# Row normalization in one ScalarE pass, gains moved to GpSimd and to the transposed copies (two-layer graph transformer, 1 core)

## Chip, core and metric

The kernel runs on one core of one Trainium2 chip. The metric is the device time of one execution in microseconds (us); smaller is better. Engines are named as in the profile: PE is TensorE (PEld its weight loads), DVE is VectorE, ACT is ScalarE, POOL is GpSimd, SP is SyncE.

## What is computed

Two layers of a graph transformer over 2708 nodes with 512 features, 8 heads of 64 and a hidden width of 2048. `x` is 2708x512, `adj` a 0/1 matrix of 2708x2708, very sparse; all values are float32. Each layer is

```
q, k, v = h @ Wq.T + bq, h @ Wk.T + bk, h @ Wv.T + bv
scores  = per head q.k / 8, and -1e9 where a node is no neighbour
ctx     = softmax(scores) @ v
h1 = layer_norm(h + ctx @ Wo.T + bo)  * ln1_g + ln1_b
h2 = layer_norm(h1 + relu(h1 @ W1.T + b1) @ W2.T + b2) * ln2_g + ln2_b
```

and `layer_norm(z)` is `(z - mean) / sqrt(variance + 1e-5)` along a row. `h2` of layer 0 is `h` of layer 1; `h2` of layer 1 is the result.

## The kernel before, in words

**Tiles and blocks.** The nodes stand in 22 tiles of 128 rows (the last has 20), ordered by how many neighbours they have. A layer works on 11 blocks of two tiles each (called blocks 0 to 10 here), in the order of the list `blocks`; the tile of 20 rows is in block 10.

**Attention** works on lists of neighbours. Keys and values of a node are one row of 1024 numbers in a DRAM table. For each neighbour slot of a tile POOL issues one indirect DMA that fetches 128 such rows (L1114, `kv<-kv_d`), into a small ring of buffers. Two slots make a chunk of attention: DVE multiplies by the queries (L1151) and sums per head (L1157, tile `sc`), ACT takes the exponential (L1170, `p<-sc`) and scales the values of one slot head by head (L1177, 8 instructions), DVE scales the other slot (L1183) and adds both to the sum (L1190). At the end of a tile ACT divides, again in 8 instructions (L1221, tile `cx`).

**Dense work** goes block by block. `attended` turns `cx` with PE, multiplies by Wo, adds the residual and normalizes: tiles `h`. `turned` transposes `h` with PE into PSUM (`flip`, tile `tp`) and ACT copies it out, adding the shift as a bias per column (L1341, `hT`). `feed_forward` (layer 0: blocks 0, 1 and 10; all of layer 1) and `feed_forward_by_seven` (layer 0: blocks 2 to 9, seven products instead of eight for W2, with partial sums of W2 in the tiles `forms`) go through the hidden width in 16 pieces, called steps 0 to 15 here: four matmuls into `pf` (L1578, L1720), a Relu by ACT into `ft` or `forms` (L1589, L1731), products with W2 three steps (or two pairs of steps) later. The result plus `h` is `z`.

**Normalization.** Most tiles use the class `Norm`. DVE adds and sums a row (`total`, L1294) and makes the negative mean `nm` (L1305). ACT squares the centred row and sums the squares (`squares`, L1311). `centred` has POOL compute the reciprocal deviation `rd` (L1318, L1320: two instructions of 128x1) while DVE forms `(z + nm) * gain` (L1321, 128x512). `scaled` has ACT multiply the row by `rd` (L1327, 128x512). The shift of the row that is kept for the residual is added by an accumulating DMA that POOL issues (`added_row`, L1330). The function `norm` does the same with other instructions, mostly on DVE, for the `h` of the first block of a layer (in layer 0 the first two) and the `z` of the last.

**What sets the order.** The order is written by hand in the loop over steps at the end of the file. While block k goes through its 16 steps, the end of block k-1 is worked off as `tail` (the generator `ended`; the table `TAILS` names the steps at which it moves on) and, in layer 0, as `behind` (`keys_values`: at step 7 the two `z` are turned and copied out as `zT`, at steps 8 and 9 the keys and values of layer 1 are projected from `zT`, L621 `k` and `v`, then the rows go to DRAM). At step 2 the shift is added to the `h` of block k. At steps 10 to 14 the next block's `attended` runs, at step 15 its `turned`. `advance` moves attention ahead by an amount that a table sets for each step. Each engine runs its instructions strictly in this written order. In layer 0, from block 2 on, `TAILS` gives the steps 3, 4, 5 and 6: squares of the first tile at 3, of the second at 4, `centred` at 5, `scaled` at 6, right ahead of the turning at 7.

**The end of layer 1.** Before the last steps of the last block the kernel makes sure that its lists held all neighbours: 22 small POOL copies (L1096, tile `checks`) at step 8, six small DVE instructions up to `held` (L1896), and at step 12 a small matmul of `held` (L1899), which stands in PE's order between the matmuls of that block. Otherwise a slower version of the whole program would run; in the runs here it doesn't.

Of the kernel before, what the change touches and what calls it, by code (L numbers as in the profile page):

```python
# [13 lines left out]
ALU = mybir.AluOpType  # L14
# [41 lines left out]
TAILS = ((0, 1, 5, 6), (3, 4, 5, 6), (0, 1, 2, 3, 5, 8))  # L56
# [428 lines left out]
def by_edges(ctx: ExitStack, tc: tile.TileContext, x, xT, adj, layers, out, redo):  # L485
# [780 lines left out]
    def norm(z, r, gain, shift=None, st=None):  # L1266
# [9 lines left out]
        nc.gpsimd.tensor_tensor(rd[:r], va[:r], mhalf[:r], ALU.pow)  # L1276
        nc.vector.scalar_tensor_tensor(
            z[:r], z[:r], mv[:r, 0:1], gain[:r], ALU.subtract, ALU.mult
        )
        if shift is None:  # L1280
            nc.vector.tensor_scalar(z[:r], z[:r], rd[:r], None, ALU.mult)
            return
        nc.vector.scalar_tensor_tensor(z[:r], z[:r], rd[:r], shift[:r], ALU.mult, ALU.add)

    class Norm:


        def __init__(self, z, r, gain, junk):
            self.z, self.r, self.gain, self.junk = z, r, gain, junk
# [25 lines left out]
        def centred(self):  # L1315
            r, z, nm = self.r, self.z, self.nm
# [4 lines left out]
            nc.vector.scalar_tensor_tensor(  # L1321
                z[:r], z[:r], nm[:r], self.gain[:r], ALU.add, ALU.mult
            )

        def scaled(self):
            r, z = self.r, self.z
            nc.scalar.activation(z[:r], z[:r], AF.Copy, scale=self.rd[:r])  # L1327
# [4 lines left out]
    def flip(z, r, to, shift=None):  # L1332
# [7 lines left out]
        for c in range(NC):  # L1340
            nc.scalar.activation(  # L1341
                to[:, c, :], tp[:, c, :r], AF.Identity, bias=shift[:, c : c + 1]
            )

    class Layer:
# [5 lines left out]
        def load_first(self):  # L1351
# [7 lines left out]
            self.unsettled = raw_columns(w, ("bv", "ln1_b"), place)  # L1359
            self.bv, self.e1 = [col[0] for col in self.unsettled]  # L1360
# [44 lines left out]
        def load_next(self):  # L1405
# [4 lines left out]
            self.unsettled += raw_columns(self.w, ("ln2_b",), place)  # L1410
            self.e2c = self.unsettled[-1][0]
# [64 lines left out]
        def attended(self, block, got, xbs=None, soon=False):  # L1476
# [16 lines left out]
            for i, xb in enumerate(xbs):  # L1493
# [8 lines left out]
                if soon:  # L1502
                    if self.n == 0 and block == blocks[0]:
                        nc.vector.tensor_tensor(h[:r], h[:r], self.bo[:r], ALU.add)
                    norm(h, r, self.g1)
                else:
                    norms.append(Norm(h, r, self.g1, xb).total(parts[-1], last))
# [6 lines left out]
            for one in norms:  # L1514
                one.centred()
# [5 lines left out]
        def turned(self, block, hs):  # L1521
            hT = dn.tile([P, NC, 2 * P], F32, tag="hT", name="hT", bufs=1)
            c0 = 0
            for g, h in zip(block, hs):
                r = size(g)
                flip(h, r, hT[:, :, c0 : c0 + r], self.e1)
# [3 lines left out]
        def feed_forward(self, block, hs, hT):  # L1530
# [81 lines left out]
            for g, a, h in zip(block, accs, hs):  # L1612
# [15 lines left out]
                else:  # L1628
                    zs.append(Norm(z, r, self.g2, a).total(a[:r], h[:r]))
                    continue  # L1630
                norm(z, r, self.g2, self.e2 if apart else None, st)
# [43 lines left out]
        def feed_forward_by_seven(self, k, block, hs, hT):  # L1675
# [93 lines left out]
            yield [Norm(z, P, self.g2, u34).total(a, z) for z, a in ((zA, a0), (zB, a1))]  # L1769
# [413 lines left out]
```

## Time and profile before

| | |
|---|---|
| two runs | 1835.44 and 1838.9 us, median 1837.17 us |
| profiled execution | 1834.85 us, of which the traced span is 1833.1 us |
| TensorE clock granted | 0.999 of full speed |
| busy in the span | PE 1807.7 us, DVE 1327.7, ACT 1050.6, POOL 919.3 |
| gathers of keys and values by POOL (L1114) | 420, 509.7 us busy |
| normalizing passes of DVE (L1321) | 78 |
| normalizing passes of ACT (L1327) | 78 |

A row of the timeline gives start, length, engine, line, operation, out<-in, the shapes and the count of what is merged in it; in brackets stands how long the engine had been idle before it and what ended that. Queue rows such as POOL's DMA instructions cost the engine's time as well.

### The profile page before, as it was taken

What the parts mean: (1) busy time and instruction counts of PE and PEld (TensorE: products, weight loads), DVE (VectorE), ACT (ScalarE), POOL (GpSimd) and SP (SyncE); (2) the same over time, 40 slices, a digit from 0 to 9 for tenths busy, and PEclk for the clock granted to TensorE, in tenths of its full rate; (3) what the DMA queues carried; (4) which work ended last, traced back from release to release, by engine and by line L of the source; (5) the groups of instructions that cost most, each with busy time, mean ns of one, the idle gap of its engine ahead of it and who ended that gap; (6) DMA issues with size and microseconds to landing.
All of it is one profiled execution on the core that took longest, in us unless ns stands there. A gap on an engine that the chain in (4) does not pass through costs nothing.

```text
span 1833.1 us, 22912 instructions
## 1 busy us (share of the span) xinstructions
PE 1807.7 (99%) x6563; PEld 1161.2 (63%) x6563; DVE 1327.7 (72%) x2271; ACT 1050.6 (57%) x3505; POOL 919.3 (50%) x929
## 2 busy tenths in 40 slices
PE   9999999999999999999999999999999999999998
PEld 4444456566777867767686644666666666666666
DVE  5986768876969778697775147867797787788732
ACT  5770436655656556565664213666676676677641
POOL 3234756645645556365551132454574566567512
PEclk9999999999999999999999999999999999999999
DMA  9997988867878787686863786955675685666511
GB/s 343 376 335 258 370 271 275 240 205 254 263 221 243 239 240 241 201 253 202 248 198 113 230 288 263 321 155 195 213 238 169 228 261 176 220 208 204 154 29 38
DMA packets 172943, 420.73 MB, mean 230 GB/s; under 512 B 19258, under 2 KB 62638, under 8 KB 172808
## 3 DMA queue, kind: packets, MB, share of 16 engines
q0 software_dynamic: 85488, 279.03, 49.1%
q1 hardware_dynamic: 77162, 118.55, 18.7%
q10 hardware_dynamic: 10158, 21.61, 3.1%
q8 instruction: 53, 0.87, 0.2%
q14 instruction: 82, 0.67, 0.1%
HBM read 338.78 MB, written 53.44 MB: 214 GB/s over the span
## 4 chain that ended last, share of the span: by engine, by line
PE 80%; issue 6%; DVE 5%; DMA 3%; ACT 3%; POOL 3%; POOLq 0%; SPq 0%; DVEq 0%; ACTq 0%
PE pf L1578 17%; PE a L1551 17%; PE pf L1720 8%; PE k L621 7%; PE v L621 7%; PE o L621 7%; PE q L621 5%; PE c L1710 4%; PE a L1710 3%; PE tp L1336 2%; DVE kv L1151 1%; ACT kv L1177 1%; DVE sc L1157 1%; POOL kv L1114 1%; DMA kv<-kv_d,listed 1%
## 5 line engine op out<-in xcount | busy, mean ns | idle before, releaser
L1114 POOL DMA_INDIRECT kv<-kv_d,listed x420 | 509.7, 1214 | 282.4 <-issue 108.3
L1578 PE MATMUL pf<-hT,w 128*128 128x256 f32 (+1 forms) x1792 | 393.1, 367 | 0.8 <-ACT ft L1589 0.7
L1578 PEld LDWEIGHTS pf<-hT,w 128*128 128x128 f32 x1792 | 323.5, 190 | 104.4 <-issue 61.0
L1551 PE MATMUL a<-w,ft 128*128 128x512 f32 x800 | 373.5, 592 | 0.1
L1177 ACT ACTIVATE kv<-kv,p 128x64 f32<-128x64 f32 x1232 | 311.0, 335 | 5.0
L1151 DVE TENSOR_TENSOR kv<-kv,q 128x1024 f32<-128x1024 f32 (+1 forms) x222 | 257.4, 1159 | 18.5 <-DMA q<-q_d,ident_i 11.7
L1157 DVE TENSOR_REDUCE sc<-kv 128x16 f32<-128x1024 f32 (+1 forms) x222 | 258.0, 1162 | 7.6
L1190 DVE TENSOR_TENSOR acc<-acc,kv 128x1024 f32<-128x1024 f32 (+2 forms) x178 | 206.3, 1159 | 58.6 <-ACT kv L1177 45.8
L1720 PE MATMUL pf<-hT,w 128*128 128x256 f32 x1024 | 232.9, 379 | 0.0
L1551 PEld LDWEIGHTS a<-w,ft 128*128 128x128 f32 x800 | 150.0, 190 | 113.0 <-issue 102.0
L1720 PEld LDWEIGHTS pf<-hT,w 128*128 128x128 f32 x1024 | 193.9, 190 | 33.3 <-issue 8.1
L1318 POOL TENSOR_SCALAR va<-sq 128x1 f32<-128x1 f32 (+1 forms) x78 | 38.2, 490 | 314.6 <-ACT xb L1311 219.5
L1170 ACT ACTIVATE p<-sc,listed 128x8 f32<-128x8 f32 x420 | 104.0, 296 | 127.8 <-DVE sc L1157 105.6
L1589 ACT ACTIVATE ft<-pf,b 128x256 f32<-128x256 f32 (+1 forms) x208 | 94.6, 458 | 105.3 <-PE pf L1578 96.6
L621 PE MATMUL o<-wo,cT 128*128 128x512 f32 x336 | 150.8, 592 | 0.0
L1183 DVE TENSOR_TENSOR kv<-kv,p 128x512 f32<-128x512 f32 (+1 forms) x178 | 123.2, 692 | 8.0 <-ACT p L1170 7.8
L1294 DVE CUSTOM_DVE_ANT_0 h<-o,xb 128x512 f32<-128x512 f32 x36 | 24.9, 691 | 129.1 <-PE o L621 105.9
L621 PEld LDWEIGHTS o<-wo,cT 128*128 128x128 f32 x336 | 63.6, 190 | 73.2 <-issue 66.5
L1731 ACT ACTIVATE ft<-pf,b 128x256 f32<-128x256 f32 x96 | 44.8, 466 | 100.0 <-PE pf L1720 95.2
L746 DVE MAX8 tops<-code 128x8 f32<-128x247 f32 (+2 forms) x242 | 78.6, 400 | 27.2 <-ACT code L741 27.2
L1330 POOL DMA_DIRECT2D h<-ln_b x86 | 83.6, 1114 | 24.5 <-PE tp L1336 21.8
L1221 ACT ACTIVATE cx<-acc,su 128x64 f32<-128x64 f32 (+1 forms) x352 | 88.3, 333 | 11.8 <-DVE su L1213 8.9
(246 smaller groups left out, 2477.2 us busy)
## 6 DMA issues: line engine op xcount, KB each, us to landing
aj<-in_adj SPq DMA_DIRECT2D x42, 677.0 KB
forms<-form_d SPq DMA_DIRECT2D x168, 128.0 KB
h<-ln_b POOLq DMA_DIRECT2D x83, 256.0 KB
kv_d<-kvs ACTq DMA_DIRECT2D x21, 512.0 KB
xg<-in_xT SPq DMA_DIRECT2D x19, 512.0 KB
w<-in_W SPq DMA_DIRECT2D x16, 512.0 KB
kv<-kv_d,listed POOLq DMA_INDIRECT x420
zT_d<-zT SPq DMA_DIRECT2D x22, 256.0 KB
```

What stands on the lines that cost most here:

```text
L621: nc.tensor.matmul(o[:r], xs(c), wm[:, c, :], start=(c == 0), stop=(c == NC - 1))
L1114: return nc.gpsimd.indirect_dma_start(out=to, out_offset=None, in_=table[:, :], in_offset=bass.IndirectOffsetOnAxis(ap=s, axis=0), bounds_ ...
L1151: nc.vector.tensor_tensor(kv[:r, :c, :DM], kv[:r, :c, :DM], self.q[:r].unsqueeze(1).to_broadcast([r, c, DM]), ALU.mult,)
L1157: nc.vector.tensor_reduce(self.sc[:r, s0 : s0 + c, :], kv[:r, :c, :DM].rearrange("p s (h d) -> p s h d", d=DK), AX.X, ALU.add,)
L1170: nc.scalar.activation(p[:r, s, :], self.sc[:r, s, :], AF.Exp, bias=minus[:r, g, s : s + 1])
L1177: nc.scalar.activation(to[:, i, hd], kv[:r, i, DM + h * DK : DM + (h + 1) * DK], AF.Copy, scale=p[:r, s0 + i, h : h + 1],)
L1183: nc.vector.tensor_tensor(to[:, 0, :].rearrange("p (h d) -> p h d", d=DK), kv[:r, 0, DM:].rearrange("p (h d) -> p h d", d=DK), p[:r, s0, : ...
L1190: nc.vector.tensor_tensor(self.acc[:r, :c, :], self.acc[:r, :c, :], kv[:r, :c, DM:], ALU.add)
L1551: nc.tensor.matmul(a[:r, cols], fts[f][:, c0 : c0 + r], self.w2[f // 2][:, f % 2, cols], start=(f == 0), stop=(f == NFC - 1),)
L1578: nc.tensor.matmul(pf[:, :w], self.w1[f // 2][:, c, f % 2 * P : f % 2 * P + P], hT[:, c, :w], start=(c == 0), stop=(c == NC - 1),)
L1710: nc.tensor.matmul(to, left, right, start=start, stop=stop)
L1720: nc.tensor.matmul(pf[:, :W], self.w1[j][:, c, f % 2 * P : f % 2 * P + P], hT[:, c, :], start=(c == 0), stop=(c == NC - 1),)
```

## The change

`Norm` no longer uses DVE for the row. `power` (in the place of `centred`) has POOL compute `rd` and also `nm * rd` (a third instruction of 128x1), and `scaled` has ACT form `z * rd + nm * rd` in one pass, with a scale and a bias per row. So `h` and `z` come out without gain and shift. Both are added where they are used: the transposed copies get the gain as a scale per column beside the shift as a bias per column (`flip`; the columns `g1c` and `g2c` are loaded and turned by PE with the others), and the rows that are kept get a multiplication by the gain on POOL (`regained`, L1334 in the changed kernel, 128x512) ahead of the accumulating DMA that they had before. `norm` loses one DVE instruction where no shift is given.

Steps move too. The squares of both tiles are issued at one step; in layer 0 `TAILS` becomes 3, 4, 5 (and 0, 1, 2 for block 1), in layer 1 `power` and `scaled` stay at steps 2 and 3. In `keys_values` both rows are multiplied and shifted at step 8 (before: one at 8, one at 9), and the stores of the rows move from step 11 to step 10.

```diff
-TAILS = ((0, 1, 5, 6), (3, 4, 5, 6), (0, 1, 2, 3, 5, 8))
+TAILS = ((0, 1, 2), (3, 4, 5), (1, 2, 3, 5, 8))
...
         nc.gpsimd.tensor_tensor(rd[:r], va[:r], mhalf[:r], ALU.pow)
+        if gain is None:
+            nc.vector.tensor_scalar(
+                z[:r], z[:r], mv[:r, 0:1], rd[:r], ALU.subtract, ALU.mult
+            )
+            return
         nc.vector.scalar_tensor_tensor(
             z[:r], z[:r], mv[:r, 0:1], gain[:r], ALU.subtract, ALU.mult
         )
-        if shift is None:
-            nc.vector.tensor_scalar(z[:r], z[:r], rd[:r], None, ALU.mult)
-            return
...
-        def centred(self):
-            r, z, nm = self.r, self.z, self.nm
+        def power(self):
+            r = self.r
             va = small.tile([P, 1], F32, tag="va", name="va")
             nc.gpsimd.tensor_scalar(va[:r], self.sq[:r], 1.0 / DM, EPS, ALU.mult, ALU.add)
             self.rd = small.tile([P, 1], F32, tag="rd", name="rd")
             nc.gpsimd.tensor_tensor(self.rd[:r], va[:r], mhalf[:r], ALU.pow)
-            nc.vector.scalar_tensor_tensor(
-                z[:r], z[:r], nm[:r], self.gain[:r], ALU.add, ALU.mult
-            )
+            nc.gpsimd.tensor_tensor(self.nm[:r], self.nm[:r], self.rd[:r], ALU.mult)
 
         def scaled(self):
             r, z = self.r, self.z
-            nc.scalar.activation(z[:r], z[:r], AF.Copy, scale=self.rd[:r])
+            nc.scalar.activation(
+                z[:r], z[:r], AF.Identity, bias=self.nm[:r], scale=self.rd[:r]
+            )
+
+    def regained(tiles, gain, row):
+
+        for z, r in tiles:
+            nc.gpsimd.tensor_tensor(z[:r], z[:r], gain[:r], ALU.mult)
+        for z, r in tiles:
+            nc.gpsimd.dma_start(out=z[:r], in_=row[:r], accum_op=ALU.add)
...
         for c in range(NC):
+            scale = 1.0 if gain is None else gain[:, c : c + 1]
             nc.scalar.activation(
-                to[:, c, :], tp[:, c, :r], AF.Identity, bias=shift[:, c : c + 1]
+                to[:, c, :], tp[:, c, :r], AF.Identity, bias=shift[:, c : c + 1], scale=scale
             )
...
             for one in norms:
                 one.squares()
-                yield
+            yield
             for one in norms:
-                one.centred()
+                one.power()
             yield
...
-            for one in norms:
-                added_row(one.z, one.r, self.e2)
+            regained([(one.z, one.r) for one in norms], self.g2, self.e2)
...
                 nc.sync.dma_start(out=zT_d[n][g], in_=zT)
-                added_row(z, r, self.e2)
+                if i == (block == blocks[-1]):
+                    regained([(z, size(g)) for g, z in zip(block, zs)], self.g2, self.e2)
                 yield
...
                 if f == (11 if k + n == 0 else 2):
-                    for g, h in zip(block, hs):
-                        added_row(h, size(g), now.e1b2)
+                    regained([(h, size(g)) for g, h in zip(block, hs)], now.g1, now.e1b2)
...
                 if n == 0 and f in (7, 8, 9, 10) and behind:
                     next(behind)
-                if n == 0 and f == 11 and behind:
-                    next(behind)
```

Two places where the order moves. First ACT in layer 0, while block 4 goes through its steps 0 to 6: `ft` and `forms` are the Relus of the steps, `u,sq` the squares of block 3's two tiles, `h<-h,rd` their last pass, `p`, `kv` and `cx` attention. Before:

```order
L1731 ACTIVATE ft<-pf,b_1157 128x256 x4
L1311 ACTIVATE u_4338,sq<-h,nm 128x512
L1731 ACTIVATE forms<-pf,b_1157 128x256
L1311 ACTIVATE u_4338,sq<-h,nm 128x512
L1170 ACTIVATE p<-sc,listed 128x8 x2
L1177 ACTIVATE kv<-kv,p 128x64 x8
L1221 ACTIVATE cx<-acc,su 128x64 x8
L1731 ACTIVATE forms<-pf,b_1157 128x256
L1170 ACTIVATE p<-sc,listed 128x8 x2
L1177 ACTIVATE kv<-kv,p 128x64 x8
L1731 ACTIVATE ft<-pf,b_1157 128x256
L1327 ACTIVATE h<-h,rd 128x512 x2
```

and with the change:

```order
L1741 ACTIVATE ft<-pf,b_1159 128x256 x4
L1313 ACTIVATE u_4358,sq<-h,nm 128x512 x2
L1741 ACTIVATE forms<-pf,b_1159 128x256
L1170 ACTIVATE p<-sc,listed 128x8 x2
L1177 ACTIVATE kv<-kv,p 128x64 x8
L1221 ACTIVATE cx<-acc,su 128x64 x8
L1741 ACTIVATE forms<-pf,b_1159 128x256
L1327 ACTIVATE h<-h,nm,rd 128x512 x2
L1170 ACTIVATE p<-sc,listed 128x8 x2
L1177 ACTIVATE kv<-kv,p 128x64 x8
L1741 ACTIVATE ft<-pf,b_1159 128x256
```

The second square and the last pass each stand one Relu sooner; the pass is now ahead of the `p` and `kv` of step 5 instead of behind those.

Second, POOL in the last block of layer 1, where `h` in the DMA rows is the row of the block before and `out` its store. Before:

```order
L1318 TENSOR_SCALAR va<-sq 128x1
L1320 TENSOR_TENSOR rd<-va,mhalf 128x1
L1318 TENSOR_SCALAR va<-sq 128x1
L1320 TENSOR_TENSOR rd<-va,mhalf 128x1
L1330 DMA h<-ln_b 128x512 x2
L1077 DMA out<-h,ident_i 2708x512 x2
L1096 COPY checks<-listed 128x1 x22
```

and with the change:

```order
L1320 TENSOR_SCALAR va<-sq 128x1
L1322 TENSOR_TENSOR rd<-va,mhalf 128x1
L1323 TENSOR_TENSOR nm<-nm,rd 128x1
L1320 TENSOR_SCALAR va<-sq 128x1
L1322 TENSOR_TENSOR rd<-va,mhalf 128x1
L1323 TENSOR_TENSOR nm<-nm,rd 128x1
L1334 TENSOR_TENSOR h<-h,ln_g 128x512 x2
L1336 DMA h<-ln_b 128x512 x2
L1077 DMA out<-h,ident_i 2708x512 x2
L1096 COPY checks<-listed 128x1 x22
```

Two instructions of 128x1 and two of 128x512 are new between the squares and the 22 copies that PE's small matmul of `held` depends on.

PE's own order stays as it was, but for three more small transposes of gain columns in all.

More of the change, by code (lines that the diff above doesn't have):

```diff
@@ L1409, in load_next @@
             place = dn.tile([P, DM], F32, tag="row", name="raw", bufs=3)
-            self.unsettled += raw_columns(self.w, ("ln2_b",), place)
-            self.e2c = self.unsettled[-1][0]
+            self.unsettled += raw_columns(self.w, ("ln2_b", "ln2_g"), place)
+            self.e2c, self.g2c = [col[0] for col in self.unsettled[-2:]]
         def preloaded(self, tiles, temp):
@@ L1504, in attended @@
                         nc.vector.tensor_tensor(h[:r], h[:r], self.bo[:r], ALU.add)
-                    norm(h, r, self.g1)
+                    norm(h, r)
                 else:
-                    norms.append(Norm(h, r, self.g1, xb).total(parts[-1], last))
+                    norms.append(Norm(h, r, xb).total(parts[-1], last))
                 hs.append(h)
@@ L1774, in ended @@
                 one.squares()
-                yield
+            yield
             for one in norms:
-                one.centred()
+                one.power()
             yield
```

23 lines of the change are left out of this document (11 added, 12 removed).

## Prediction

> **What bounds the kernel now.** First the page's busy times, then who released PE where it waited (totals, times, longest), then two stretches: a block of layer 0 and one of layer 1.
>
> ```profile
> PE 1807.7 (99%) x6563; PEld 1161.2 (63%) x6563; DVE 1327.7 (72%) x2271; ACT 1050.6 (57%) x3505; POOL 919.3 (50%) x929
> ...
> PE tp L1336 <- ACT h L1327: 9.1, 8, 1.8
> PE k L621 <- ACT zT L1341: 2.6, 2, 2.3
> PE k L621 <- ACT kvs L1819: 2.1, 1, 2.1
> ...
> PE a L1710 <- DMA forms<-form_d: 0.2, 1, 0.2
> ...
> 572.00:649.00 77.00, 75.82 (x312) 56.65 (x311) 61.57 (x103) 48.88 (x177) 44.66 (x43) 1.00 0.79 246
> 1277.00:1341.00 64.00, 64.00 (x228) 41.41 (x227) 50.34 (x68) 44.85 (x164) 39.14 (x35) 1.00 0.64 207
> ```
>
> PE is busy 1807.7 of 1833.1 us, and its order does not change. All that can be won lies in its 25.4 us of idleness; the three rows that end with ACT hold 13.8 of it. In layer 1 PE does not wait at all (64.00 of 64), so time saved there on DVE or spent on POOL is worth nothing while it stays hidden. In layer 0 a block loses 1.2 of 77 us, and the first row says where: the transposes of `z` at step 7 wait for ACT's last pass (L1327), eight times, 9.1 us. That is what the earlier pass aims at. Two per cent of the median are 36.7 us, more than all of PE's idleness, and about what a measurement of this kernel can tell from no change.
>
> **What a layer 0 block shows.** Block 4's steps 4 to 8, ACT's rows first, then DVE's, then PE's:
>
> ```profile
> 557.11 0.47 ACT L1731 ACTIVATE forms<-pf,b 128x256 f32<-128x256 f32 x1 [0.55 <-PE pf L1720]
> 557.48 0.71 ACT L1311 ACTIVATE u<-h,nm 128x512 f32<-128x512 f32 x1
> 562.53 0.46 ACT L1731 ACTIVATE forms<-pf,b 128x256 f32<-128x256 f32 x1
> 563.40 2.02 ACT L1177 ACTIVATE kv<-kv,p 128x64 f32<-128x64 f32 x8
> 565.69 1.32 ACT L1327 ACTIVATE h<-h,rd 128x512 f32<-128x512 f32 x2
> 570.17 0.30 ACT L1170 ACTIVATE p<-sc,listed 128x8 f32<-128x8 f32 x1 [0.73 <-DVE kv L1151]
> 570.73 2.16 ACT L1341 ACTIVATE zT<-tp,ln_b 128x128 f32<-128x128 f32 x8
> ...
> 561.89 1.41 DVE L1321 SCALAR_TENSOR_TENSOR h<-h,nm,ln_g 128x512 f32<-128x512 f32 x2
> 566.39 1.23 DVE L1190 TENSOR_TENSOR acc<-acc,kv 128x1024 f32<-128x1024 f32 x1
> 569.45 0.69 DVE L1157 TENSOR_REDUCE sc<-kv 128x8 f32<-128x512 f32 x1
> ...
> 566.45 1.27 PE L1336 MATMUL tp<-ident,h 128*128 128x128 f32 x8 [1.18 <-ACT h L1327]
> 570.58 1.89 PE L1720 MATMUL pf<-hT,w 128*128 128x256 f32 x8
> 572.30 1.45 PE L621 MATMUL k<-wk,zT 128*128 128x512 f32 x3
> ```
>
> PE waits 1.18 us for the pass that starts at 565.69. But PE's next need is `zT`: the projection `k` at 572.30 needs the first four of ACT's eight copies that start at 570.73, done at about 571.8 (half of 2.16 later). So there are only 0.5 us between that copy and PE. If PE comes 1.18 us earlier, it stands before `k` instead, unless ACT comes earlier too.
>
> **The change part by part.**
>
> *The pass one step sooner.* In ACT's queue it now stands ahead of the `p` and `kv` of step 5. Step by step in block 4: the second square fills the idle 0.55 before the Relu at 557.11, so the Relu at 562.53 starts at about 561.9; the pass follows at 562.3 and lasts 1.5 (1.32, and 0.1 a tile for a second row operand, below); then come the step's `p` (0.5) and `kv`, which started at 563.40 and now starts at 564.3 and ends at 566.2. DVE's addition at 566.39 needs that `kv`. Hence DVE, freed of L1321 (1.41 us at 561.89), gains nothing there: it adds at 566.3, and `sc` (569.45 before) comes 0.1 earlier, the `p` at 570.17 and `zT` too, at 570.6; four dearer copies take 1.5, and PE's `k` starts at about 572.1 instead of 572.30. Of 1.18 us some 0.2 are left: the wait moves from the transposes to `k`. Bounds per block: -0.4 (if DVE's addition comes no earlier and the copies are dearer still) and 1.18. Blocks 3 to 6 have the same waits and steps: 4 x 0.2 = 0.8 us. In block 2, with the longest wait (1.8), `p` and `cx` stand otherwise and I take half, 0.9. Block 1 has what is left of the 9.1, 0.2.
>
> *DVE's pass removed.* It counts where DVE is the one who is late, in blocks 7 and 8:
>
> ```profile
> 792.58 1.36 DVE L1321 SCALAR_TENSOR_TENSOR h<-h,nm,ln_g 128x512 f32<-128x512 f32 x2
> 801.87 0.49 ACT L1170 ACTIVATE p<-sc,listed 128x8 f32<-128x8 f32 x2 [1.37 <-DVE sc L1157]
> 804.68 2.15 ACT L1341 ACTIVATE zT<-tp,ln_b 128x128 f32<-128x128 f32 x8
> 805.84 1.55 PE L621 MATMUL k<-wk,zT 128*128 128x512 f32 x3 [2.32 <-ACT zT L1341]
> ...
> 893.15 0.59 ACT L1819 COPY kvs<-v 128x512 f32<-128x512 f32 x1 [1.40 <-issue]
> 893.79 1.55 PE L621 MATMUL k<-wk,zT 128*128 128x512 f32 x3 [2.07 <-ACT kvs L1819]
> ```
>
> Before `k` at 805.84 ACT had waited 1.37 us for `sc`, and DVE had spent 1.36 on L1321 ahead of it. Without it `zT` comes up to 1.36 earlier, less 0.4 for the dearer copies and 0.2 for the pass; POOL's multiplications may take more of it back (below). The two stalls at transposes and `k` are in series, so PE gains what `zT` gains: between -0.6 and 1.2, I take 0.5, and the same in block 8, whose `k` waits for a buffer that DVE releases to the copy at 893.15. Sum of layer 0: 0.2 + 0.9 + 0.8 + 1.0 = 2.9 us.
>
> *The second operand on ACT.* The trace has no pass with both a scale and a bias per row. The nearest rows are a copy without and a Relu with one such operand:
>
> ```profile
> L1762 ACT COPY u<-c 128x256 f32<-128x256 f32 x8 | 2.9, 363 | 11.5 <-PE c L1710 11.5
> L1731 ACT ACTIVATE ft<-pf,b 128x256 f32<-128x256 f32 x96 | 44.8, 466 | 100.0 <-PE pf L1720 95.2 <-issue 4.6
> L959 POOL TENSOR_TENSOR kvs<-kvs,bk 128x512 f32<-128x512 f32 x20 | 25.4, 1271 | 52.8 <-ACT kvs L957 48.1 <-issue 4.7
> ...
> 1057.42 0.28 PE L1382 MATMUL pr<-ident,raw 4*128 4x4 f32 x2
> ```
>
> 363 against 466 ns: 0.1 us for the first. Bounds for the second: 0 and 0.1; I take 0.1. It lies on the path in the four copies before `k` (0.4) and in the pass, and is counted there. The copies of `hT` have not held up a first product in this trace and stay covered unless they take the whole of the products with W2 ahead of it.
>
> *POOL.* 86 multiplications of 128x512; the same form took 1271 ns (L959), 109 us in all, and 78 of 128x1. POOL has 32 us of a layer 0 block free (44.66 of 77 busy) and needs some 7 more: four multiplications and four small ones. Behind them in its queue stand gathers and stores of keys. They mostly wait for DVE to release buffers, so a delay of 2.5 us twice a block ends in that wait; if it did not, DVE would get its rows late and PE stand before `k` as above. SP's store of the rows waits for the accumulating DMA, and its loads of `forms` behind it have had at most 0.2 us of PE waiting. Taken: 0.
>
> *The end of layer 1.* Here POOL is on the path:
>
> ```profile
> 1792.33 0.69 ACT L1311 ACTIVATE a<-h,nm 128x512 f32<-128x512 f32 x1
> 1794.06 0.55 POOL L1320 TENSOR_TENSOR rd<-va,mhalf 128x1 f32<-128x1 f32 x1
> 1796.49 1.77 POOL L1330 DMA_DIRECT2D h<-ln_b  x2 [1.89 <-ACT fts L1589]
> 1800.08 1.10 POOL L1077 DMA_INDIRECT out<-h,ident_i  x1 [1.82 <-DMA h<-ln_b]
> 1802.64 2.67 POOL L1096 COPY checks<-listed 128x1 f32<-128x1 f32 x22
> ...
> 1806.09 0.16 DVE L1896 TENSOR_REDUCE held<-flags 128x1 f32<-128x6 f32 x1
> 1806.30 0.09 PEld L1899 LDWEIGHTS pr<-held,ones 128*1 128x1 f32 x2 [0.79 <-DVE held L1896]
> ```
>
> The second `rd` ends at 1794.6, the two accumulating DMAs start at 1796.49, the stores wait for their landing, the 22 copies follow, DVE makes `held` at 1806.25, and PE's weights for L1899 load at 1806.30, 0.79 us after they could: no cover at all. With the change both squares follow the Relu of step 1, so the second starts at about 1793.2 instead of 1792.33, 0.9 later; two small instructions of some 0.3 are new (between a `va` of 0.19, quoted below, and the `rd` of 0.55), so the second `nm` is there at about 1796.1, 1.5 later than that `rd`; two multiplications of 1.27 end at 1798.7, and the DMAs start at about 1798.9. Everything behind them moves by 2.4 us, and PE's matmuls behind L1899 with it. Bounds: 2.1 (1.5 + 2.54, with all of the 1.89 us that POOL idled before the DMA to absorb them) and 4.0 (with none of it). I take 2.4, near the lower, because that idleness was a wait for ACT's pass, which is over by then.
>
> *Small transposes.* Three more; two took 0.28 us (1057.42), so 0.14 each: 0.4.
>
> **Sum.** 1834.85 - 2.9 + 2.4 + 0.4 = 1834.8 on the profiled execution's own time (span 1833.1 and 1.75 around it). That execution lies 2.3 below the median of the two runs, 1837.17; the three together average 1836.4, so the forecast for a median is 1836.4 - 0.1, say 1836 us: **no change that can be measured**.
>
> **A rule against the change.** The nearest rows for GpSimd beside DVE are two of POOL's smallest instructions in block 8, and the DVE instruction that ran beside the second:
>
> ```profile
> 867.32 0.19 POOL L1318 TENSOR_SCALAR va<-sq 128x1 f32<-128x1 f32 x1 [1.91 <-ACT u L1311]
> 868.18 1.22 DVE L1151 TENSOR_TENSOR kv<-kv,q 128x1024 f32<-128x1024 f32 x1
> 869.03 0.42 POOL L1318 TENSOR_SCALAR va<-sq 128x1 f32<-128x1 f32 x1 [0.87 <-ACT u L1311]
> ```
>
> The first, ahead of that product, took 0.19 us. The second took 0.42 and ended at 869.45, when DVE's product of two tiles ended (869.40). So POOL waits for a DVE instruction that reads two tiles; whether DVE also waits for a long POOL multiplication no row shows, since L959 ran beside DVE instructions with one input.
> [...]
>
> **Rivals.**
>
> *DVE is held up by the multiplications; slower.* Place: layer 0, step 2 (rows `h`) and step 8 (rows `z`). Price: the pair at step 2 holds DVE up by up to 2 x 1.27 = 2.54 us, and the removed L1321 gives back 1.4; 1.1 are left, with 0.4 for dearer copies 1.5 a block, in blocks 2 to 9 12 us. It decides as soon as DVE loses more than it is given back, between its work at step 2 and `sc` at step 6. For it: the wait in the other direction that the rows above show, and DVE's 61.57 of 77 us. Against: several DVE instructions of step 2 read PSUM, and POOL can fall between them. 1834.85 + 12 + 2.8 = 1850 us.
>
> *The waits at the transposes go and nothing takes their place; faster.* If ACT's `kv` is not what DVE waits for, 9.1 us are won, at most also the 4.7 of the `k` rows: 1834.85 - 9.1 + 2.8 = 1828.6, with all of them 1824; I give it 1827. Against it: the 0.5 us between `zT` and `k`.
>
> *The pass doesn't come sooner.* If POOL's `power` at step 4 stands behind gathers that wait, ACT's pass waits for `nm` at step 5 and all behind it on ACT. Then nothing is won: 1834.85 + 2.8 = 1837.7, on the median's footing 1839 us. For it: POOL works in order, and gathers that wait for DVE stand in the same queue. Against: `power` is issued a whole step ahead of the pass, and its six small instructions need 2 to 3 us.
>
> **How the numbers follow.** Forecast 0.50, DVE held up 0.22, waits gone 0.20, pass not sooner 0.08. The forecast's own range is 1831 to 1841. The range of all: from 1826 (most of the waits gone) to 1848 (DVE held up in most blocks) leaves out the outer parts of two rivals, about 0.15. Faster by over 2% would need more than PE's idleness: 0.01. Slower by over 2% would need 37 us, three times the rival's price, or 4.6 us in each of eight blocks: 0.03. Within: 0.96.
>
> **What would show it.** Right: the row of transposes waiting for ACT's `h` is gone from PE's waits, and `k` waits for `zT` in blocks 2 to 8 by 0.5 to 2 us each; PE's busy time grows by under 1 us; the L1899 matmul waits 2 to 3 us for `held`; layer 1 has no other wait; four `zT` copies take 1.5 us. Wrong: PE waits add up to under 8 us (rival two), DVE's two-input instructions in layer 0 are longer than before or follow POOL's multiplications (rival one), or ACT idles before L1327 for POOL (rival three).

## The result, and the profile after

| | before | after |
|---|---|---|
| runs, us | 1835.44, 1838.9 | 1864.99, 1866.02 |
| median, us | 1837.17 | 1865.51 |
| ratio, 95% interval | | 1.0154, 1.0111 to 1.0198 |
| span of the profiled execution, us | 1833.1 | 1863.3 |

The changed kernel is 28 us slower. The forecast was 1836 us, and the range ended at 1848. The page's busy times of the changed kernel, and then who released PE where it waited (total, times, longest):

```profile
PE 1819.2 (98%) x6566; PEld 1164.0 (62%) x6566; DVE 1342.5 (72%) x2188; ACT 1080.6 (58%) x3505; POOL 1012.7 (54%) x1093
```

```profile
PE k L621 <- ACT zT L1351: 14.0, 8, 5.0
PE k L621 <- DVE kvs L1823: 5.2, 3, 2.4
PE k L621 <- ACT kvs L1828: 4.7, 1, 4.7
PE o L621 <- ACT cT L1351: 2.3, 4, 1.0
PE pr L1908 <- DVE held L1905: 1.8, 1, 1.8
...
PE pr L1392 <- DVE q L1072: 1.5, 1, 1.5
```

The row of transposes that wait for ACT's `h` (9.1 us before) is gone, as forecast. PE's idleness, the span less its busy time, nevertheless grew from 25.4 to 44.1 us, and PE itself is busy 11.5 us longer with the same matmuls and three small ones. So there are two losses: waits, nearly all at `k`, and a slower PE.

**Where the waits come from.** DVE has 78 passes of 0.70 us (55 us) less to do, and is busy 14.8 us more. Its groups by shape in the changed kernel (busy, mean ns), and behind the dots two of them in the kernel before:

```profile
L1157 DVE TENSOR_REDUCE sc<-kv 128x16 f32<-128x1024 f32 x196 | 239.1, 1220 | 6.7
L1190 DVE TENSOR_TENSOR acc<-acc,kv 128x1024 f32<-128x1024 f32 x154 | 199.2, 1293 | 76.2 <-ACT kv L1177 66.1
L1183 DVE TENSOR_TENSOR acc<-kv,p 128x512 f32<-128x512 f32 x42 | 42.4, 1009 | 12.6 <-ACT p L1170 12.6
L1198 DVE TENSOR_TENSOR acc<-acc 128x512 f32<-128x512 f32 x42 | 35.2, 838 | 0.1
L1697 DVE TENSOR_TENSOR forms<-ft 128x128 f32<-128x128 f32 x40 | 24.5, 614 | 29.1 <-PE c L1720 27.3 <-ACT cx L1221 1.2 <-ACT ft L1741 0.4
...
L1183 DVE TENSOR_TENSOR acc<-kv,p 128x512 f32<-128x512 f32 x42 | 29.3, 697 | 3.4 <-ACT p L1170 3.4
L1687 DVE TENSOR_TENSOR forms<-ft 128x128 f32<-128x128 f32 x40 | 11.2, 281 | 25.0 <-PE c L1710 10.1 <-issue 9.3 <-ACT ft L1731 3.2
```

The reduction of one tile (L1157) takes 1220 ns, as before. What is longer are instructions that read two tiles, though not all of them (`h<-c,h`, L1776, takes 0.41 us beside a pair, at 793.20, the same as elsewhere): the 128x128 addition L1697 (L1687 before) takes 614 ns instead of 281, L1183 (`acc<-kv,p`) 1009 instead of 697. The timeline shows how such a mean arises. POOL's pair of step 8 of block 4, and the DVE instructions beside it; the last row is of another place:

```profile
582.45 2.51 POOL L1334 TENSOR_TENSOR h<-h,ln_g 128x512 f32<-128x512 f32 x2
...
581.50 0.68 DVE L1198 TENSOR_TENSOR acc<-acc 128x512 f32<-128x512 f32 x1
582.66 2.46 DVE L1697 TENSOR_TENSOR forms<-ft 128x128 f32<-128x128 f32 x1
585.16 0.29 DVE L1698 TENSOR_TENSOR ft<-ft 128x128 f32<-128x128 f32 x1
...
793.53 1.79 DVE L1777 TENSOR_TENSOR h<-u,h 128x256 f32<-128x256 f32 x1
```

A DVE addition that takes 0.28 us alone starts behind POOL's first multiplication and ends only after the second (585.12 against 584.96): it is held for the whole pair. The last row stands beside a pair of step 2, in block 7, 792.52 to 795.02: an addition of 0.42 us took 1.79. Few instructions carry the loss: 35 are each 1.0 to 3.0 us longer than the median of the same instruction in the kernel without the multiplications (e1, below).

**Where the slower PE comes from.** The projection with the longest wait, and the windows around it (span, PE busy, granted clock, share and GB/s of DMA):

```profile
816.25 6.14 PE L621 MATMUL k<-wk,zT 128*128 128x512 f32 x8 [4.97 <-ACT zT L1351]
```

```profile
812.00:816.00 4.00, 0.00 (x0) 0.80 0.87 269
816.00:820.00 4.00, 3.75 (x5) 0.50 0.92 296
820.00:824.00 4.00, 4.00 (x10) 0.85 0.98 389
```

After 4.97 us without a matmul the granted clock is 0.50, and the eight matmuls of `k`, 3.60 to 3.70 us where the clock does not fall, take 6.14. Cutting the span into windows of 4 us and adding busy time x (1 - clock) over the nine with work under 0.985 gives 8.1 us of PE's 11.5; the other 3.4 are not accounted for. Before, no window with work was under 0.985.

### The profile page after: what moved, and what is told of

It reads as the page before. It is cut to its first block, busy times and chain, and to the rows that moved or that the text cites. A ratio compares the mean times of both kernels' runs of the same rounds, so it can differ in the third digit from the quotient of the medians.

```text
span 1863.3 us, 23092 instructions
## 1 busy us (share of the span) xinstructions
PE 1819.2 (98%) x6566; PEld 1164.0 (62%) x6566; DVE 1342.5 (72%) x2188; ACT 1080.6 (58%) x3505; POOL 1012.7 (54%) x1093
## 4 chain that ended last, share of the span: by engine, by line
PE 68%; DVE 13%; ACT 9%; issue 6%; POOL 2%; DMA 1%; DVEq 0%; POOLq 0%; ACTq 0%
PE pf L1588 14%; PE a L1561 14%; PE o L621 8%; PE k L621 7%; PE v L621 7%; PE q L621 7%; PE pf L1730 4%; ACT kv L1177 3%; DVE kv L1151 3%; DVE sc L1157 3%; PE c L1720 2%; PE a L1720 2%; PE tp L1345 2%; DVE acc L1190 1%; ACT cx L1221 1%
## 5 line engine op out<-in xcount | busy, mean ns | idle before, releaser
L1114 POOL DMA_INDIRECT kv<-kv_d,listed x420 | 516.0, 1229 | 266.5 <-issue 109.2
L1151 DVE TENSOR_TENSOR kv<-kv,q 128x1024 f32<-128x1024 f32 (+1 forms) x222 | 264.2, 1190 | 15.3 <-DMA q<-q_d,ident_i 10.7
L1190 DVE TENSOR_TENSOR acc<-acc,kv 128x1024 f32<-128x1024 f32 (+2 forms) x178 | 218.4, 1227 | 77.0 <-ACT kv L1177 66.1
L1157 DVE TENSOR_REDUCE sc<-kv 128x16 f32<-128x1024 f32 (+1 forms) x222 | 257.9, 1162 | 7.6
L1320 POOL TENSOR_SCALAR va<-sq 128x1 f32<-128x1 f32 (+1 forms) x78 | 22.2, 284 | 272.5 <-ACT xb L1313 187.5
L1183 DVE TENSOR_TENSOR kv<-kv,p 128x512 f32<-128x512 f32 (+1 forms) x178 | 138.5, 778 | 24.6 <-ACT p L1170 24.1
L1334 POOL TENSOR_TENSOR h<-h,ln_g 128x512 f32<-128x512 f32 (+1 forms) x86 | 109.6, 1296 | 23.6 <-PE tp L1345 22.8
L621 PE MATMUL k<-wk,zT 128*128 128x512 f32 x168 | 81.9, 633 | 23.9 <-ACT zT L1351 14.0
```

Of the source, the lines that this page charges most:

```text
L621: nc.tensor.matmul(o[:r], xs(c), wm[:, c, :], start=(c == 0), stop=(c == NC - 1))
L1114: return nc.gpsimd.indirect_dma_start(out=to, out_offset=None, in_=table[:, :], in_offset=bass.IndirectOffsetOnAxis(ap=s, axis=0), bounds_ ...
L1151: nc.vector.tensor_tensor(kv[:r, :c, :DM], kv[:r, :c, :DM], self.q[:r].unsqueeze(1).to_broadcast([r, c, DM]), ALU.mult,)
L1157: nc.vector.tensor_reduce(self.sc[:r, s0 : s0 + c, :], kv[:r, :c, :DM].rearrange("p s (h d) -> p s h d", d=DK), AX.X, ALU.add,)
L1183: nc.vector.tensor_tensor(to[:, 0, :].rearrange("p (h d) -> p h d", d=DK), kv[:r, 0, DM:].rearrange("p (h d) -> p h d", d=DK), p[:r, s0, : ...
L1190: nc.vector.tensor_tensor(self.acc[:r, :c, :], self.acc[:r, :c, :], kv[:r, :c, DM:], ALU.add)
```

## The experiments

Theory: POOL's multiplications hold up DVE's instructions that read two tiles, and PE's longer stalls cost clock on top. "The port" in the expectations is the author's name for whatever the two engines share there; the runs show the hold-up, and no run shows what it is that they share. Rivals: POOL's queue, made later by the multiplications; or ACT with its dearer copies and moved pass. All gains in the inputs are 1, so a kernel without a gain has the same data. Ratios are against the kernel before on the same chip. Its medians there lay between 1836.3 and 1837.3 us, so a difference of two medians from different chips can be off by about 1 us.

| | median, us | ratio, 95% interval |
|---|---|---|
| without the multiplications (e1) | 1838.16 | 1.0, 0.9987 to 1.0013 |
| memsets instead (e2) | 1840.78 | 1.0017, 1.0005 to 1.0029 |
| kernel before, pass sooner alone (e3) | 1834.32 | 0.9984, 0.9974 to 0.9994 |
| multiplications by DVE (e4) | 1848.46 | 1.0058, 1.0041 to 1.0076 |
| multiplications of step 2 only (e5) | 1853.33 | 1.0088, 1.0071 to 1.0105 |
| multiplications of step 8 only (e6) | 1849.84 | 1.0072, 1.0055 to 1.0089 |
| e1, copies with one operand (e7) | 1837.42 | 1.0004, 0.9995 to 1.0014 |
| e3, `k` later, check earlier (e8) | 1845.86 | 1.0046, 1.003 to 1.0063 |
| e3, check at step 1 (e9) | 1832.83 | 0.9977, 0.9968 to 0.9986 |
| a DMA between the multiplications (e10) | 1867.25 | 1.017, 1.0149 to 1.0191 |
| e7, no third column (e11) | 1834.39 | 0.999, 0.9981 to 0.9999 |
| POOL reads one tile, not two (e12) | 1844.67 | 1.0044, 1.0028 to 1.0061 |

**Without the multiplications (e1).**

```diff
     def regained(tiles, gain, row):
 
         for z, r in tiles:
-            nc.gpsimd.tensor_tensor(z[:r], z[:r], gain[:r], ALU.mult)
-        for z, r in tiles:
             nc.gpsimd.dma_start(out=z[:r], in_=row[:r], accum_op=ALU.add)
```

> The changed kernel without the 86 multiplications of 128x512 on POOL (left out: the gain of the rows kept for the residual). Theory (the port): each multiplication keeps DVE's two-input instructions waiting while it reads its rows; without them DVE's busy time falls from 1342.5 to about 1265 us, the mean of L1697's 128x128 additions from 614 to about 280 ns, and the time to 1833 to 1838 us. Rival (POOL's queue: the multiplications only make the gathers behind them late): the same time. Rival (ACT: the copies with two operands and the moved pass cost the 28 us): the time stays above 1855 us.

1838.16 us: the 86 multiplications cost 27 us, and ACT, whose work is unchanged, is not what costs. The page, then two of DVE's groups:

```profile
PE 1813.4 (99%) x6566; PEld 1165.2 (63%) x6566; DVE 1270.7 (69%) x2188; ACT 1079.0 (59%) x3505; POOL 903.6 (49%) x1007
```

```profile
L1198 DVE TENSOR_TENSOR acc<-acc 128x512 f32<-128x512 f32 x42 | 28.7, 683 | 0.1
L1695 DVE TENSOR_TENSOR forms<-ft 128x128 f32<-128x128 f32 x40 | 11.2, 281 | 35.1 <-PE c L1718 30.5 <-ACT ft L1739 3.7 <-DMA form_d<-forms 0.9
```

DVE's busy time is 71.8 us lower with the same 2188 instructions, and the additions (L1695 here) are back at 281 ns: of 109.6 us of multiplications two thirds were also DVE's waiting. (The changed kernel and e1 ran on different occasions; by their ratios the difference is 28 us.)

**Memsets in their place (e2).**

```diff
-            nc.gpsimd.tensor_tensor(z[:r], z[:r], gain[:r], ALU.mult)
+            for _ in range(6):
+                nc.gpsimd.memset(ones, 1.0)
```

> The changed kernel with each multiplication on POOL replaced by six memsets of 128x128 into a tile that nobody reads then (left out: the gain of the rows kept for the residual). They keep POOL's queue busy for 6 x 0.205 = 1.23 us in place of 1.27, but read nothing. Theory (the port): DVE is not held up, the time is within 5 us of the kernel without multiplications, 1833 to 1842 us. Rival (POOL's queue): gathers are as late as in the changed kernel, 1858 us or more. Rival (ACT): above 1855 us as well, but then the kernel without multiplications is too.

```profile
PE 1809.8 (98%) x6566; PEld 1163.4 (63%) x6566; DVE 1270.1 (69%) x2188; ACT 1078.4 (59%) x3505; POOL 1004.2 (55%) x1523
...
L1335 POOL MEMSET ones<- 128x128 f32 x516 | 106.2, 206 | 27.3
```

POOL is as busy as in the changed kernel (106.2 against 109.6 us at this place), and the time is 1840.78 us, 2.6 over e1, with DVE busy 1270.1. So not POOL's time, but its reading, is what costs; its queue is worth some 2.6 us, and no more than 7.7 at the far ends of both intervals. The memsets are also six short instructions in place of one long, but a hold by each would show in DVE's busy time, and that is as in e1 (1270.7). By the changed kernel, e1 and e2, POOL holds DVE up where it reads two tiles (DVE 71.8 us busier than in e1), and not where it only writes (0.6 us less than in e1). In the changed kernel DVE waits to the end: the addition above ends 0.16 us behind POOL's pair. Coming first did not help: 10 of the 35 long DVE instructions start 0.2 to 0.7 us ahead of POOL's pair by the records and end behind it all the same, while all but five of POOL's 86 multiplications take 1.25 to 1.29 us. Whether POOL's recorded starts are late is open.

**The halves (e5, e6).** In e5 the z rows of step 8 get only their DMA, in e6 the h rows of step 2:

```diff
-                    regained([(z, size(g)) for g, z in zip(block, zs)], self.g2, self.e2)
+                    for g, z in zip(block, zs):
+                        added_row(z, size(g), self.e2)
```

```diff
-                    regained([(h, size(g)) for g, h in zip(block, hs)], now.g1, now.e1b2)
+                    for g, h in zip(block, hs):
+                        added_row(h, size(g), now.e1b2)
```

> The changed kernel in which only the rows h (step 2) and the last output rows are multiplied on POOL; the z rows of layer 0 at step 8 are not (left out: their gain). The first rival of the prediction put its whole price on the pair at step 2 and none on the pair at step 8. By it this kernel is as slow as the changed one, 1855 us or more. Theory now: both pairs hold up DVE, the one at step 8 by more (2.2 us in the block looked at, against about 1.4 for step 2, of which the removed DVE pass gives some back); then this kernel takes 1840 to 1852 us, and less than the one with step 8 alone.

> The changed kernel in which only the z rows of layer 0 (step 8) and the last output rows are multiplied on POOL; the rows h at step 2 are not (left out: their gain). By the prediction's first rival, which priced step 2 alone, 1840 us or less. Theory now: the pair at step 8 stands just ahead of the sums that make the next sc and costs some 2 us a block in eight blocks, 1848 to 1858 us, more than step 2 alone. If DVE has slack that one pair fits into and two don't, both halves lie under 1843 us.

1853.33 and 1849.84 us, 15.2 and 11.7 over e1. They add up: 26.9 against 27.3 for both (e5 and e6 ran on another chip than e1). No slack swallows one of them. The 20 output rows of layer 1 are multiplied in both, and so counted twice. That step 8 would cost more than step 2 was wrong; e5 also holds the pairs of layer 1. Up to the start of the last `k` of layer 0 the profiled execution of e5 is 10.5 us behind e1's, that of e6 7.8, that of the changed kernel 19.9. Over the whole span the changed kernel is 23.2 behind. Against the same instructions in e1, DVE is held 41 us up to that `k` and 34 behind it (the single instructions that grew; all of DVE's busy time makes it 72), so in layer 1 most of the hold-up costs nothing: only 3.3 of the 23.2 us are lost there.

**By DVE itself (e4).**

```diff
-            nc.gpsimd.tensor_tensor(z[:r], z[:r], gain[:r], ALU.mult)
+            nc.vector.tensor_tensor(z[:r], z[:r], gain[:r], ALU.mult)
```

> The changed kernel with the same 86 multiplications at the same places of the program, but on DVE (0.69 us each, 59 us in all, against the 55 us of DVE's pass that the change removed). Theory (the port): nothing of POOL reads beside DVE for long, so the time falls to 1833 to 1842 us although DVE's own work grows. Rival (ACT): above 1855 us. If DVE's own work at steps 2 and 8 is as bad as being held up there, 1850 us or more.

```profile
PE k L621 <- ACT zT L1351: 13.6, 8, 4.8
PE k L621 <- ACT kvs L1828: 5.2, 3, 4.4
```

1848.46 us: 17 better than on POOL, but not the 1833 to 1842 of the first expectation, and just short of the 1850 of the last. DVE is busy 1320.6 us, 7 less than before the change, and yet 11 us are lost: what counts is where the work stands. Steps 2 and 8 lie ahead of the products and sums for `sc`, on which ACT and then `zT` wait; PE's waits at `k` fit this, and no run moved the work elsewhere to show it.

**The pass sooner alone (e3).** The kernel before with nothing but the steps changed:

```diff
-TAILS = ((0, 1, 5, 6), (3, 4, 5, 6), (0, 1, 2, 3, 5, 8))
+TAILS = ((0, 1, 2), (3, 4, 5), (1, 2, 3, 5, 8))
...
             for one in norms:
                 one.squares()
-                yield
+            yield
```

> The kernel before with nothing changed but the steps: both squares at one step and the last pass one step sooner, in the same places as in the changed kernel; arithmetic, DVE's pass and ACT's operands as before. The prediction's first term: the wait of 9.1 us at the transposes goes, but most of it comes back as waits of k for zT; PE's idleness falls by 1 to 4 us, 1833 to 1837 us. Rival (nothing takes their place): about 9 us less, 1828 us. Rival (ACT: moving the pass is what costs): above 1845 us.

```profile
PE k L621 <- ACT zT L1341: 7.0, 6, 3.9
PE k L621 <- ACT kvs L1819: 2.6, 2, 2.5
PE pr L1899 <- DVE held L1896: 2.6, 1, 2.6
```

1834.32 us, 3.0 less than before. Where the transposes had waited 9.1 us, `k` now waits 7.0 for `zT` (2.6 before). This is the wait that moves. The third row is new as well.

**One operand, and no third column (e7, e11).** e7 is e1 with `scale = 1.0` in `flip`; e11 is e7 without loading and turning `ln1_g` and `ln2_g` (of e11's edit only the first place is shown):

```diff
-            scale = 1.0 if gain is None else gain[:, c : c + 1]
+            scale = 1.0
```

```diff
-            self.unsettled = raw_columns(w, ("bv", "ln1_b", "ln1_g"), place)
-            self.bv, self.e1, self.g1c = [col[0] for col in self.unsettled]
+            self.unsettled = raw_columns(w, ("bv", "ln1_b"), place)
+            self.bv, self.e1 = [col[0] for col in self.unsettled]
```

> The changed kernel without the multiplications on POOL and without the scale per column in the turned copies, which so have one operand as before (left out: all gains of the normalizations in the blocks' usual path). Theory: what is left between the kernel without multiplications (1838 us) and the one with the pass sooner alone (1834 us) are the dearer copies, 4 x 0.09 us ahead of k and as much ahead of the first product in each block of layer 0; so 1833 to 1836 us here. Rival: it is the third POOL instruction and the pass with two operands, or the end of layer 1; then 1837 us or more.

> The changed kernel without multiplications and without the scale per column, and now also without loading and turning the gains as columns (left out: all gains of the normalizations in the blocks' usual path). In the trace of the changed kernel the third small transpose at 188 us waits 1.53 us for DVE to release a buffer, which the prediction priced at 0.14. Theory: 1.5 to 2 us less than with the columns, 1835 to 1836 us. Rival (the time before the first block is set elsewhere): the same time as with them, 1837.4 us.

e7 takes 1837.42 us, not distinguishable from e1: the dearer copies, 464 instead of 375 ns each for `zT`, leave no measurable trace in the time. e11 takes 1834.39, 3.0 less, more than expected; by the ratios it is 2.6, and the two intervals still touch. The changed kernel shows why; the three columns at 186 us, then the windows behind them:

```profile
186.32 0.28 PE L1392 MATMUL pr<-ident,temp 4*128 4x4 f32 x2
188.14 0.22 PE L1392 MATMUL pr<-ident,temp 4*128 4x4 f32 x1 [1.53 <-DVE q L1072]
```

```profile
188.00:192.00 4.00, 3.86 (x7) 0.72 0.69 215
192.00:196.00 4.00, 4.00 (x9) 0.86 0.94 299
```

The third small transpose waits 1.53 us for a buffer that DVE's copy of `q` still reads, and in this execution, as in that of e5, the clock fell behind it. e7's profiled execution has a wait of 1.33 us there and no fall; e11's has neither, and PE is busy without a break. So a wait of 1.3 to 1.5 us goes, and what the rest of the 3.0 is, if it is more than noise, was not shown. e11 is as fast as e3: DVE's pass removed, ACT's pass with two operands and the third small POOL instruction together are worth nothing that can be measured.

**A DMA in between (e10).**

```diff
         for z, r in tiles:
             nc.gpsimd.tensor_tensor(z[:r], z[:r], gain[:r], ALU.mult)
-        for z, r in tiles:
             nc.gpsimd.dma_start(out=z[:r], in_=row[:r], accum_op=ALU.add)
```

> The changed kernel with the accumulating DMA of the first row issued between the two multiplications instead of behind both: the same instructions, but POOL reads no rows for about 1 us between them. In the trace one DVE addition of 0.28 us took 2.46 us beside a pair of 2.51 us. Theory (DVE waits for whatever stands back to back and gets in at the first gap): no DVE instruction is held for more than 1.3 us, but every multiplication still holds one, and 40 to 70 us of hold-up stay of the 72; 1853 to 1863 us. If the hold-up is by the single instruction only, nothing changes, 1865 us.

1867.25 us, not distinguishable from the changed kernel, and DVE is busy 1355.4, so the theory's hope that less would be held was wrong. Both multiplications of a pair in block 7:

```profile
825.73 1.27 POOL L1334 TENSOR_TENSOR h<-h,ln_g 128x512 f32<-128x512 f32 x1
827.99 1.64 POOL L1334 TENSOR_TENSOR h<-h,ln_g 128x512 f32<-128x512 f32 x1
...
825.08 2.08 DVE L1698 TENSOR_TENSOR forms<-forms,ft 128x128 f32<-128x128 f32 x1
828.07 2.64 DVE L1151 TENSOR_TENSOR kv<-kv,q 128x1024 f32<-128x1024 f32 x1
```

An addition of 0.28 us takes 2.08, a product of 1.22 takes 2.64, and each ends behind its multiplication. Each multiplication holds the instruction with two tiles that stands beside it here; with a gap between them they simply hold two different instructions.

**POOL reads one tile (e12).**

```diff
-            nc.gpsimd.tensor_tensor(z[:r], z[:r], gain[:r], ALU.mult)
+            nc.gpsimd.tensor_scalar(z[:r], z[:r], 1.0, None, ALU.mult)
```

> The changed kernel with each multiplication of two tiles on POOL replaced by a multiplication of the same tile by the constant 1 (left out: the gain of the rows kept for the residual). POOL then reads one tile in place of two. Theory (any reading of SBUF by POOL keeps DVE's two-input instructions waiting for as long as the instruction lasts): DVE's busy time stays 40 us or more above the 1270 of the kernel without multiplications, and the time above 1850 us, more or less as POOL's instruction is longer or shorter than 1.27 us. Rival (only POOL's second input needs what DVE needs): DVE's busy time about 1270 us and the time 1838 to 1843 us, as with memsets.

```profile
PE 1812.5 (98%) x6566; PEld 1162.4 (63%) x6566; DVE 1301.1 (71%) x2188; ACT 1079.6 (59%) x3505; POOL 1043.3 (57%) x1093
...
582.80 3.01 POOL L1334 TENSOR_SCALAR h<-h 128x512 f32<-128x512 f32 x2
...
582.28 0.61 DVE L1697 TENSOR_TENSOR forms<-ft 128x128 f32<-128x128 f32 x1
582.93 0.68 DVE L1698 TENSOR_TENSOR ft<-ft 128x128 f32<-128x128 f32 x1
583.53 0.28 DVE L1699 TENSOR_TENSOR forms<-forms,ft 128x128 f32<-128x128 f32 x1
583.91 0.51 DVE L1700 TENSOR_TENSOR forms<-ft,forms 128x128 f32<-128x128 f32 x1
```

1844.67 us, between the two expectations. DVE is busy 1301.1 us: 30 us of hold-up beside 135 of POOL, where two inputs made 72 beside 110. Of four additions the first ends just behind POOL's start, and three more got through while the pair of 3.01 us ran; each was held 0.4 us at most, and no DVE instruction of the kernel as much as 1 us. By the expectation's theory they would have waited for all of it, as the addition beside POOL's two-input pair did (2.46 us). Why POOL holds DVE less with one input was not looked into.

**`k` a step later (e8), and the check earlier (e8, e9).** On top of e3; all of it is e8, the last two lines alone are e9:

```diff
-                if n == 0 and f in (7, 8, 9, 10) and behind:
+                if n == 0 and f in (7, 9, 10, 11) and behind:
                     next(behind)
-                if n == 0 and f == 11 and behind:
+                if n == 0 and f == 10 and behind:
                     next(behind)
...
-                if last and not more and f == 8:
+                if last and not more and f == 1:
                     checked()
```

> The kernel before with the pass sooner, the projections k and v of both tiles one step later (steps 9 and 10 in place of 8 and 9, the stores of keys still at step 10), and the check of the lists at step 1 of the last block in place of step 8. Theory (the wait went from the transposes to k because zT has only one step of cover): with a step more PE stands at neither, and the end of layer 1 doesn't wait for held; of the 12 to 13 us that PE waits there with the pass sooner alone 8 to 10 are won, 1824 to 1829 us. Rival (the lateness is of the whole chain through DVE and only moves on): PE waits as long for cT or kvs at step 10, 1832 us or more.

```profile
PE k L621 <- ACT kvs L1819: 15.3, 6, 3.3
...
PE k L621 <- ACT zT L1341: 0.2, 1, 0.2
```

1845.86 us: the rival was right. The wait for `zT` is gone (0.2 us), but now the second tile's `k` waits for the copy of the first one's values, 15.3 us. In block 3:

```profile
509.50 0.59 ACT L1819 COPY kvs<-v 128x512 f32<-128x512 f32 x1 [2.39 <-PE pf L1720]
...
508.20 1.22 DVE L1190 TENSOR_TENSOR acc<-acc,kv 128x1024 f32<-128x1024 f32 x1
509.53 0.69 DVE L1814 TENSOR_TENSOR kvs<-k,bk 128x512 f32<-128x512 f32 x1
```

ACT idled 2.39 us ahead of that copy although its input was long there, and it started when DVE's addition ended (509.42). That `kvs` waits for a buffer of the ring which this addition reads fits, and is argued from the times only.

> The kernel before with the pass sooner, and with the check of the lists at step 1 of the last block in place of step 8. With the pass sooner alone (1834.3 us) the small matmul of held still waits 2.6 us behind POOL's stores and copies. Theory: the copies need nothing that is late at step 1, the wait goes, 1831 to 1833 us, 4 to 6 us under the kernel before. Rival (the wait stands for other work at the end, which then waits instead): 1834 us.

1832.83 us, ratio 0.9977 (0.9968 to 0.9986): the row of `held` is gone from PE's waits, as expected. This is the lowest median here, under both the kernel before and the changed one; against e3 (0.9974 to 0.9994) the intervals overlap, so what the wait's going is worth in time is not shown.

## Why the prediction was wrong

**The step that failed** is the term "Taken: 0" for POOL. It reckoned with gathers behind the multiplications, and e2 shows that this is worth some 2.6 us. What the multiplications do to DVE was left to a rival with 0.22. The runs put them at 27 us, nearly the whole of the 28: DVE was held for 72 us, and PE's waits at `k` grew from 4.7 to 23.9.

**The rival had the mechanism, and half of the price.** That a multiplication holds DVE for its whole 1.27 us was the author's estimate, and no row of before showed it; in the changed kernel an addition of 0.28 us beside a pair of 2.51 took 2.46, and all 86, 109.6 us of POOL, held DVE up for 72. The rival took the pair at step 2 at 12 us in layer 0; e5 lost 15.2 in all, 10.5 of them in layer 0 in the profiled executions. The pair at step 8 it named, but did not price; e6 lost 11.7. With the second pair priced like the first, the rival's 1850 would have been 1862. The reason given against it, that POOL can fall between DVE's instructions, does not hold: DVE arrives while POOL runs, and e10 (1867.25 us) shows that gaps do not help. The two small rows quoted there (0.42 us of POOL beside DVE's product, 0.19 without) showed that one of the two engines can wait for the other; that no row showed DVE waiting was no reason to give it less than half the chance of the forecast.

**The pass sooner** was right in mechanism: the wait moves to `k`. That its total fits, 2.9 forecast for layer 0 and 3.0 measured in e3, is partly luck. The 2.9 hold 1.0 for DVE's pass in blocks 7 and 8, which e3 keeps (and e11, without it, is no faster than e3; 1 us is about what their intervals can tell apart). And the 3.0 are of the whole kernel: in the profiled executions the last `k` of layer 0 starts 4.0 us sooner in e3, and 2.6 of it are lost again at the end of layer 1. From the starts of `k`, blocks 5 and 6 gained 1.5 each, and block 8 lost 1.

**The second operand** was right: the copies of `zT` went from 373 to 463 ns, ACT's pass from 710 to 803.

**Small transposes:** 0.4 forecast for their own duration; the third waited 1.53 us for a buffer, and e7 less e11 is 3.0 (2.6 by the ratios).

**The end of layer 1:** PE waited 1.8 us for `held`, 2.4 forecast. But e3, without any multiplication, waits 2.6 there, and e2 3.4, so the reason was not shown to be the multiplications. In e3 the second store starts 3.5 us after the first, where 1.5 lay between them before:

```profile
1796.73 1.10 POOL L1077 DMA_INDIRECT out<-h,ident_i  x1 [1.82 <-DMA h<-ln_b]
1800.26 1.02 POOL L1077 DMA_INDIRECT out<-h,ident_i  x1 [2.43 <-DMA h<-ln_b]
```

The later store waits for its accumulating DMA to land. Why that took longer stays open. With no cover at all any lateness shows, and moving the check (e9) removes the wait.

**"PE's busy time grows by under 1 us"** failed: 11.5, of which 8.1 by the clock. **"Layer 1 has no other wait"** failed too: the row of `o` behind `cT`, 2.3 us, lies there, and e5, which keeps the pairs of layer 1, has it while e1 doesn't. That time spent on POOL in layer 1 costs nothing while it stays hidden did hold in the main: of 34 us of hold-up there, 3.3 us were lost.

## What to carry to other kernels

Work moved to an idle engine was not free here, because it held up the engine that it relieved: 55 us of DVE's passes became 110 us of POOL, and held DVE up for 72. What that costs depends on the slack around it: 41 us of it in layer 0 cost some 20, 34 in layer 1 some 3. Before pricing a move at nothing, look at which instructions will run beside it, and price every place where it is issued, not only the one that comes to mind first. And a stall on the bounding engine moved by a step is not a stall removed: of 9.1 us at the transposes, the whole kernel won 3.

## What the runs showed of the hardware

PE's clock after a stall, in the profiled executions of all fourteen kernels, for PE's waits of 1.5 us and more in the span from 330 us on (the two falls at 188 us, behind waits of 1.53 and 1.56 us, lie ahead of it); "fell" means a granted clock under 0.95 in the four us behind the wait:

| wait, us | waits | clock fell |
|---|---|---|
| 1.5 to 2.0 | 12 | 1 |
| 2.0 to 2.7 | 24 | 6 |
| 2.7 to 4.0 | 16 | 13 |
| over 4.2 | 9 | 9 |

A fall makes the eight matmuls of `k` 5.1 to 6.8 us long instead of 3.7, so a stall of 5 us costs 7 or more (in the changed kernel 4.97 of wait and, with `k` at 6.14 us, 2.4 of longer matmuls). Behind the longest waits the granted clock is 0.50. The length of the wait alone does not decide: two waits of 2.03 us in e10 end in a clock of 0.79, then 0.50, with `k` at 5.40 us, and in 1.00 with `k` at 3.70. 13 of the 29 falls follow waits of 1.8 to 3.3 us, and all nine waits of 4.3 to 5.0 us have a fall. What decides is open.
